# A long convolution as Toeplitz matmuls on one core: 128-row blocks against 64-row blocks in four tiles of the array

## The chip, the cores and the metric

The kernel runs on one core of a Trainium2 chip. The metric is the device time of one execution in microseconds (us), taken as the median of several runs. Three runs of the kernel before gave 2309.24, 2312.29 and 2312.61 us; the median is 2312.29 us.

## The reference

The input `x` has 32 batch entries, 64 channels (tokens of the later layers) and 1024 positions, all in fp32. Four residual layers follow each other. The first is the one that changes here: a state-space convolution along the 1024 positions, one filter per channel, with a mask by length.

```python
K = _get_kernel(log_dt, C, log_A_real, A_imag, Lq)      # one filter of 1024 taps per channel
y = irfft(rfft(u, n=2*Lq) * rfft(K, n=2*Lq)[None])[..., :Lq]   # causal convolution
y = y + u * D[:, None]
x = x + y * (arange(Lq)[None, :] < length[:, None])[:, None, :]
x = x + einsum('bsi,boi->bso', x, weight1[adapter_ids1])        # 1024 x 1024 weight per batch entry
x = x + einsum('bij,bkj->bik', x, weight2[adapter_ids2])        # the same with another table
x = x + lora_ffn(x)                                             # gate, up, silu, down, each with LoRA
```

## The kernel before, in words

The batch is cut into four chunks of eight entries. For every chunk the kernel runs sixteen adapter products (eight entries, two layers) and then the feed-forward layer. The convolution is done once, in the beginning, for all 32 entries: the part of chunk 0 is added to `x` in SBUF at once (L1419), the parts of the other chunks go to DRAM (`cd`, L1423) and are read back later.

**The filters.** The function `kernels(g)` makes the filters of a group of 4 or 8 channels from sines, cosines and exponentials on ScalarE, VectorE and GpSimd, and a small matmul (`pk`, L1346). ScalarE copies the result out (L1364) and stores it in a DRAM tile `kp` by a DMA on its own queue (L1366). Nine groups are made; the first two before the convolution starts, the others one at a time from within it, through `more()`, which `convolve` calls as `between()`.

**The convolution.** `convolve(kp, row, ha, between)` is called sixteen times, each for `HA = 4` channels. In this text a call is one of these sixteen. In a call, SyncE's queue (SP) first loads `uf`, the inputs of the four channels with the positions of a 128-block reversed (L1376). Then, for two channels at a time, it loads `hk` (L1385): 128 rows of 1024 numbers for each channel, read from `kp` in such a way that row p starts p numbers later. Every 128 columns of this table are one square Toeplitz block. The convolution of a channel is eight matmuls (L1404), one for each distance d between an output block and an input block: a 128 x 128 block as weights, and (8 - d) x 32 columns of `uf` as the moving operand, so 256, 224, ... 32 columns, all summed in PSUM. VectorE multiplies two channels' sums by the mask into `tmp` (L1172), GpSimd adds chunk 0's part to `x` and stores the rest.

**The weights that come early.** The adapters' weights come as 128 x 1024 tiles of 512 KB; chunk 0 needs 128 of them. While the convolution runs, SP also loads such tiles for chunk 0: `fetch(n)` issues the next n of them (L170). They go to places of their own (16 `early` tiles, 4 in the second `x` buffer, called `x_early`, and 7 `late` ones that open when the last filters are made) and to 9 rotating buffers `wa`, 36 in all. `fetch(8)` stands in the first call; later calls fetch one to two tiles each, 28 by the end, and the last eight are issued behind the last table. When the adapters begin, each rotating buffer is loaded again as soon as TensorE has used it.

**Order.** TensorE's order is the program's (it is scheduled by hand). SP's queue is in the order of the program too: the load of a `uf` buffer waits for the call two before, that of an `hk` buffer for the matmuls that last read it, and what stands behind it in the queue waits with it. The adapters of chunk 0 (L304) start when GpSimd has added the last call's result to `x`.

In the trace, an fp32 matmul stands as two instructions, each with its own weight load.

Of the kernel before, what the change touches and what calls it, by code (L numbers as in the profile page):

```python
# [9 lines left out]
F32 = mybir.dt.float32  # L10
# [9 lines left out]
P = 128  # L20
B, H, L = 32, 64, 1024
NS = 64
KT = L // P
# [8 lines left out]
MB = 4  # L32
MG = 2
NG = FM // MG
EARLY = 16
LEFT_AT = 11
LATE = 7
FIRST_LOADS = 8
MORE_LOADS = 3
ROTATING = 9  # L40
HA = 4
SEG = 2
# [10 lines left out]
KROW = P + L  # L53
# [23 lines left out]
def kernel(  # L77
# [55 lines left out]
    epool = first.enter_context(tc.tile_pool(name="epool", bufs=1, side="right"))  # L133
    early = [epool.tile([P, L], F32, tag=f"e{i}", name=f"early{i}") for i in range(EARLY)]
    early += [
# [995 lines left out]
def convolution(tc, cst, consts, xt, xf, ssm, lens, x0, cd, ps_tile, fetch, places):  # L1131
# [10 lines left out]
    nc = tc.nc  # L1142
    with ExitStack() as ctx:
# [5 lines left out]
        s3 = ctx.enter_context(tc.tile_pool(name="s3", bufs=3))  # L1149
# [14 lines left out]
        def small():  # L1164
            n_small[0] += 1
            return s1.tile([P, H], F32, tag=f"sm{n_small[0]}", name=f"sm{n_small[0]}")
# [4 lines left out]
        def tt(o, a, b, op):  # L1171
            nc.vector.tensor_tensor(o, a, b, op)  # L1172
            return o
# [80 lines left out]
        x, y = small(), small()  # L1254
# [6 lines left out]
        t, em, ep = small(), small(), small()  # L1261
# [110 lines left out]
        def convolve(kp, row, ha, between):  # L1372


            uf = s3.tile([P, HA, KT, B], F32, tag="uf", name=f"uf{ha}", bufs=2)
            nc.sync.dma_start(uf, xf[:, ha : ha + HA])  # L1376
            if ha == 0:
                fetch(FIRST_LOADS)
            tmp = g0_2.tile([P, HA, KT * B], F32, tag="tmp", name=f"tmp{ha}")
            for i in range(0, HA, 2):  # L1380
                hk = s3.tile([P, 2, L], F32, tag="hk", name=f"hk{ha + i}")

                for j in range(0, 2, 1 if ha == 0 else 2):
                    n = 1 if ha == 0 else 2
                    nc.sync.dma_start(  # L1385
                        hk[:, j : j + n],
                        bass.AP(
                            tensor=kps.tensor,
                            offset=kp[row + i + j : row + i + j + 1, 1:2].offset,
                            ap=[[1, P], [KROW, n], [1, L]],  # L1390
                        ),
                    )

                first, last = ha <= HA * MORE_LOADS, ha > H - HA * MORE_LOADS
                if ha and i == 0:
                    fetch(1 + first)
                elif ha and last:
                    fetch(1)
                if i:
                    between()  # L1400
                ps = ps_tile(f"pc{ha + i}").rearrange("p (i t) -> p i t", i=2)
                for j in range(2):
                    for d in range(KT):
                        nc.tensor.matmul(  # L1404
                            ps[:, j, d * B :],
                            hk[:, j, d * P : (d + 1) * P],
                            uf[:, i + j, : KT - d, :].rearrange("p k b -> p (k b)"),
                            start=(d == 0),
                            stop=(d == KT - 1),
                        )  # L1410
                tt(
                    tmp[:, i : i + 2, :],
                    ps,
                    maskf.unsqueeze(1).to_broadcast([P, 2, KT * B]),
                    ALU.mult,
                )
            xv = x0.rearrange("p k (b h) -> p k b h", h=H)[:, :, :, ha : ha + HA]
            tv = tmp.rearrange("p i (k b) -> p k b i", b=B)[:, :, :BC, :]
            nc.gpsimd.tensor_tensor(xv, xv, tv, ALU.add)  # L1419
            co = g0.tile([P, NCK - 1, HA * KT, BC], F32, tag="co", name=f"co{ha}")  # L1420
            tv = tmp.rearrange("p i (k c b) -> p c (i k) b", k=KT, b=BC)[:, 1:]
            nc.gpsimd.tensor_copy(co, tv)
            nc.gpsimd.dma_start(  # L1423
                cd.rearrange("c p g e -> p c g e")[:, :, ha // HA],
                co.rearrange("p c i b -> p c (i b)"),
            )
# [14 lines left out]
        maskf = mask.rearrange("p k b -> p (k b)")  # L1441
        for g, n in enumerate(GROUPS):
            h0 = sum(GROUPS[:g])

            def more():
                if len(ready) < min(g + 3, len(GROUPS)):
                    ready.append(kernels(len(ready)))
                    if len(ready) == len(GROUPS):
                        making.close()
                        places()  # L1450

            for i in range(0, n, HA):
                convolve(ready[g], i, h0 + i, more)
# [20 lines left out]
def _layouts(np, v):  # L1474
    cont = np.ascontiguousarray

    x = v["x"]

    xt = x.reshape(NCK, TC, KT, P).transpose(3, 0, 2, 1)

    xf = x.reshape(B, H, KT, P)[..., ::-1].transpose(3, 1, 2, 0)

    def states(a):
        return np.concatenate([a.T, a.T])
# [58 lines left out]
    for i, (m0, m1) in enumerate(BLOCKS):  # L1543
        n = 2 * (m1 - m0)
        ad[:, i, :, :n] = a[:, :, :, m0:m1].reshape(NE, P, n, R)
    left = left.reshape(P + REST, NE, R).transpose(1, 0, 2)
    n = 2 * BLOCKS[0][1]
# [71 lines left out]
```

## Time and profile before

| what | value |
|---|---|
| median of 3 runs | 2312.29 us |
| span of the profiled execution | 2313.8 us |
| TensorE busy | 2249.8 us (97%) |
| TensorE weight loads busy | 1868.0 us (81%) |
| DMA, mean over the span | 296 GB/s |
| first table `hk` issued | 25.14 us |
| adapters of chunk 0 begin in the chain of waits | 195.76 us |
| last adapter matmuls of chunk 0 end | 329.83 us |
| matmuls of the convolution (L1404) | 1024 instructions, 153.3 us busy |
| tables `hk` | 30 loads of 1024 KB and 4 of 512 KB |

The profiled execution's span is 1.5 us over the median of the runs. Times inside a stage are read from the start of this span. A busy TensorE isn't TensorE at its peak, since matmuls are pipelined and their ends are modelled; what a stage costs is read from its start and end, and from the wait that ends last in it.

### The profile page before, as it was taken

To read this page: it belongs to the slowest core of one execution; us is meant where nothing else is said; L and a number is where in the kernel's file an instruction comes from. 1 tells how busy PE (TensorE), PEld (TensorE's weight loads), DVE (VectorE), ACT (ScalarE), POOL (GpSimd) and SP (SyncE) were. 2 spreads that over 40 slices of the span, in tenths; PEclk is the share of its full clock that TensorE was granted. 3 is DMA by queue.
4 is the path that set the end of the run, shared out by engine and by line. 5 is a ranking of instruction groups with operands and counts; after the bars stand their busy time and mean duration, and the time that the engine had idled before them with its cause. 6 is when DMAs were issued, how large, how long until landed. Compare 5 with 4: busy or idle time off the path is not lost.

```text
span 2313.8 us, 53743 instructions
## 1 busy us (share of the span) xinstructions
PE 2249.8 (97%) x21706; PEld 1868.0 (81%) x21706; DVE 1320.6 (57%) x2791; ACT 380.0 (16%) x822; POOL 270.6 (12%) x388
## 2 busy tenths in 40 slices
PE   5999989999999999999999999999999999999999
PEld 4996557787777789688778889688769889799998
DVE  7511127567446776546535676646535676477585
ACT  4300001011001112111102212121102212121220
POOL 3423003111101121000000011000000011100000
PEclk9999999999999999999999999999999999999999
DMA  8999997879997957879997957879997947285582
GB/s 306 354 370 394 407 403 280 317 289 354 365 343 293 350 174 258 304 285 360 350 357 279 358 167 265 297 292 358 355 351 288 363 152 276 87 298 203 191 280 68
DMA packets 201802, 684.96 MB, mean 296 GB/s; under 512 B 26178, under 2 KB 28482, under 8 KB 201042
## 3 DMA queue, kind: packets, MB, share of 16 engines
q1 hardware_dynamic: 169714, 590.77, 69.5%
q0 software_dynamic: 25184, 82.37, 9.6%
q10 hardware_dynamic: 6656, 8.39, 1.0%
q8 instruction: 171, 2.80, 0.5%
q14 instruction: 77, 0.63, 0.1%
HBM read 614.02 MB, written 67.40 MB: 295 GB/s over the span
## 4 chain that ended last, share of the span: by engine, by line
PE 78%; DMA 14%; issue 5%; DVE 2%; POOL 1%; POOLq 0%; SPq 0%; ACT 0%; DVEq 0%
PE pq L664 28%; PE po L1063 22%; PE pa L304 11%; DMA wa<-in_w 7%; PE pc L1404 5%; PE pf L573 5%; PE pr L797 3%; DMA wa<-sums 2%; DMA sums<-kept 1%; PE pe L456 1%; DMA hk<-kp 1%; PE pl_d L427 1%; DMA kp<-ks 1%; DMA wf<-in_wg 0%; DMA wr<-in_wr 0%
## 5 line engine op out<-in xcount | busy, mean ns | idle before, releaser
L304 PE MATMUL pa<-wa,x 128*32 128x256 f32 x7760 | 449.1, 381 | 19.3 <-DMA wa<-in_w 16.8
L664 PE MATMUL pq<-xd,wa 128*128 128x128 f32 x3360 | 415.9, 275 | 1.3 <-DMA wa<-sums 0.9
L304 PEld LDWEIGHTS pa<-wa,x 128*32 128x32 f32 x7760 | 241.8, 110 | 209.9 <-DMA wa<-in_w 49.1
L664 PEld LDWEIGHTS pq<-xd,wa 128*128 128x128 f32 x3360 | 395.0, 192 | 2.3 <-DMA wa<-sums 2.2
L664 PE MATMUL pq<-xd,wb 128*128 128x128 f32 x2520 | 324.1, 276 | 0.6 <-DVE x L316 0.4
L664 PEld LDWEIGHTS pq<-xd,wb 128*128 128x128 f32 x2520 | 300.7, 192 | 4.7 <-DVE x L316 0.6
L314 DVE STREAM_TRANSPOSE y<-pa 128x512 f32<-128x512 f32 x64 | 45.9, 717 | 286.6 <-PE pa L304 286.6
L1063 PE MATMUL po<-act,wd 128*128 128x256 f32 x640 | 168.6, 386 | 0.0
L1404 PE MATMUL pc<-uf,hk 128*128 128x256 f32 (+7 forms) x1024 | 153.3, 312 | 12.2 <-DMA hk<-kp 9.5
L1063 PE MATMUL po<-actd,s 128*128 128x256 f32 x640 | 164.2, 379 | 0.0
L1063 PE MATMUL po<-actd,wd 128*128 128x256 f32 x640 | 164.2, 379 | 0.0
L1404 PEld LDWEIGHTS pc<-uf,hk 128*128 128x128 f32 x1024 | 148.4, 195 | 16.6 <-issue 7.9
L355 POOL DMA_INDIRECT bgu<-in_bgu,rows x44 | 51.4, 1168 | 924.0 <-PE pe L456 827.2
L573 PE MATMUL pf<-xd,wf 128*128 128x256 f32 x640 | 150.9, 381 | 0.0
L1063 PEld LDWEIGHTS po<-act,wd 128*128 128x128 f32 x640 | 117.8, 190 | 29.9 <-issue 14.6
L482 DVE TENSOR_TENSOR s<-wd 128x256 f32<-128x256 f32 x80 | 33.8, 423 | 184.1 <-PE po L1063 184.0
L573 PEld LDWEIGHTS pf<-xd,wf 128*128 128x128 f32 x640 | 121.2, 191 | 17.4
L1063 PEld LDWEIGHTS po<-actd,s 128*128 128x128 f32 x640 | 121.6, 190 | 16.5
L1063 PEld LDWEIGHTS po<-actd,wd 128*128 128x128 f32 x640 | 121.6, 190 | 16.5
L1095 ACT COPY uo<-po 128x256 f32<-128x256 f32 x48 | 17.9, 373 | 622.3 <-PE po L1063 620.2
L573 PE MATMUL pf<-xd,s 128*128 128x256 f32 x480 | 115.9, 385 | 3.9 <-DVE up L607 2.7
L573 PEld LDWEIGHTS pf<-xd,s 128*128 128x128 f32 x480 | 91.0, 191 | 20.0 <-DVE up L607 4.4
(235 smaller groups left out, 2566.4 us busy)
## 6 DMA issues: line engine op xcount, KB each, us to landing
wa<-in_w SPq DMA_DIRECT2D x485, 512.0 KB, 7.0
wa<-sums SPq DMA_DIRECT2D x210, 512.0 KB, 5.8
wb<-parts SPq DMA_DIRECT2D x120, 384.0 KB, 5.3
wd<-in_wd SPq DMA_DIRECT2D x80, 512.0 KB, 7.0
wb<-in_wq SPq DMA_DIRECT2D x90, 384.0 KB, 5.9
hk<-kp SPq DMA_DIRECT2D x30, 1024.0 KB, 8.8
sums<-kept POOLq DMA_DIRECT2D x30, 1024.0 KB, 7.2
wf<-in_wg SPq DMA_DIRECT2D x20, 512.0 KB, 7.1
```

The source lines that it names most:

```text
L304: nc.tensor.matmul(acc[i * S : (i + 1) * S, s * 256 : (s + 1) * 256], xs[c][:, kt, lo + s * S : lo + (s + 1) * S], wt[:, i * 256 : (i + 1) ...
L314: nc.vector.transpose(y, acc)
L355: nc.gpsimd.indirect_dma_start(out=t, out_offset=None, in_=table, in_offset=bass.IndirectOffsetOnAxis(ap=at_, axis=0),)
L427: nc.tensor.matmul(ps[pair(j)], at[:, i, pair(j)], x_i[:, 2 * H * j : 2 * H * (j + 1)], start=(i == 0), stop=(i == n - 1),)
L456: nc.tensor.matmul(ps[:, at_ * 2 * H : (at_ + 1) * 2 * H], bt[pair(j), g], tms[table][pair(j)], start=(g == 0), stop=True, skip_group_chec ...
L482: nc.vector.tensor_add(s1, a21, a22)
L573: nc.tensor.matmul(ps, ws[j][:, kt, :], xb[j][:, kt, :], start=start and kt == 0, stop=kt == KH - 1, skip_group_check=True,)
L664: nc.tensor.matmul(ps[:, to * TQ : (to + 1) * TQ], w[i][:, k, :], xb[:, j, SLOT[i], k, :], start=start and k == 0 and to == 0, stop=k == K ...
L797: nc.tensor.matmul(ps, wts[i][:, kt, :], xs[c][:, kt, :], start=(kt == 0), stop=(kt == KT - 1),)
L1063: nc.tensor.matmul(pss[j], *term, start=(s0 == m0 and i == 0 and home[j] % 2 == 0), stop=(end and i == len(terms) - 1 and not late), skip_ ...
L1095: nc.scalar.copy(u1, p1)
L1404: nc.tensor.matmul(ps[:, j, d * B :], hk[:, j, d * P : (d + 1) * P], uf[:, i + j, : KT - d, :].rearrange("p k b -> p (k b)"), start=(d == ...
```

## The change

A block becomes 64 x 64 numbers. A table `hk` now holds a pair of channels (`PAIR = 2`): rows 0 to 63 are one channel's table, rows 64 to 127 the other's, so that a channel's table has 64 rows of 1024 numbers instead of 128. It is loaded by two DMAs for each pair, one for each half of the rows. There are four such buffers of 4 KB per row instead of three of 8 KB. The input `uf` is laid out on the host to fit: its row halves hold the two channels, and for each the even and the odd 64-blocks apart.

For each pair the matmuls run over 16 distances e, two halves q of the output rows, and two channels r. A matmul has 64 rows of weights and 64 columns of weights and stands in one of four tiles of the array: r picks the row half, q the column half. The two channels' sums go to two PSUM banks (`banks[r]`), which hold both pairs of a call. There are 62 matmuls for a pair where there were 16. The mask products run for both banks at the end of the call.

The freed memory gives two more `early` tiles (18), so that 38 weights are held. `fetch(2)` stands in each call behind the first, ahead of the second pair's table; with `fetch(8)` in the first call that issues all 38 within the convolution.

```diff
-EARLY = 16
+EARLY = 18
-MORE_LOADS = 3
+PAIR = 2
+HP = P // PAIR
...
-            uf = s3.tile([P, HA, KT, B], F32, tag="uf", name=f"uf{ha}", bufs=2)
-            nc.sync.dma_start(uf, xf[:, ha : ha + HA])
+            uf = s3.tile([P, HA // PAIR, 2, KT * B], F32, tag="uf", name=f"uf{ha}", bufs=2)
+            nc.sync.dma_start(uf, xf[:, ha // PAIR : (ha + HA) // PAIR])
             if ha == 0:
                 fetch(FIRST_LOADS)
             tmp = g0_2.tile([P, HA, KT * B], F32, tag="tmp", name=f"tmp{ha}")
-            for i in range(0, HA, 2):
-                hk = s3.tile([P, 2, L], F32, tag="hk", name=f"hk{ha + i}")
-
-                for j in range(0, 2, 1 if ha == 0 else 2):
-                    n = 1 if ha == 0 else 2
+            halves = [slice(r * HP, (r + 1) * HP) for r in range(PAIR)]
+            banks = [ps_tile(f"pc{ha}_{r}").rearrange("p (i t) -> p i t", i=HA // PAIR) for r in range(PAIR)]
+            for i in range(HA // PAIR):
+                hk = s3.tile([P, L], F32, tag="hk", name=f"hk{ha}_{i}", bufs=4)
+                for r in range(PAIR):
+                    h = row + PAIR * i + r
                     nc.sync.dma_start(
-                        hk[:, j : j + n],
+                        hk[halves[r]],
                         bass.AP(
                             tensor=kps.tensor,
-                            offset=kp[row + i + j : row + i + j + 1, 1:2].offset,
-                            ap=[[1, P], [KROW, n], [1, L]],
+                            offset=kp[h : h + 1, HP + 1 : HP + 2].offset,
+                            ap=[[1, HP], [1, L]],
                         ),
                     )
-
-                first, last = ha <= HA * MORE_LOADS, ha > H - HA * MORE_LOADS
                 if ha and i == 0:
-                    fetch(1 + first)
-                elif ha and last:
-                    fetch(1)
+                    fetch(2)
                 if i:
                     between()
-                ps = ps_tile(f"pc{ha + i}").rearrange("p (i t) -> p i t", i=2)
-                for j in range(2):
-                    for d in range(KT):
-                        nc.tensor.matmul(
-                            ps[:, j, d * B :],
-                            hk[:, j, d * P : (d + 1) * P],
-                            uf[:, i + j, : KT - d, :].rearrange("p k b -> p (k b)"),
-                            start=(d == 0),
-                            stop=(d == KT - 1),
-                        )
+                for e in range(PAIR * KT):
+                    for q in range(PAIR):
+                        k0 = (e - q + 1) // 2 if e > q else 0
+                        if k0 == KT:
+                            continue
+                        for r in range(PAIR):
+                            nc.tensor.matmul(
+                                banks[r][halves[q], i, k0 * B :],
+                                hk[halves[r], e * HP : (e + 1) * HP],
+                                uf[halves[r], i, (q - e) % 2, : (KT - k0) * B],
+                                start=(e == 0),
+                                stop=(e == PAIR * (KT - 1) + q),
+                                skip_group_check=True,
+                            )
+            for r in range(PAIR):
                 tt(
-                    tmp[:, i : i + 2, :],
-                    ps,
-                    maskf.unsqueeze(1).to_broadcast([P, 2, KT * B]),
+                    tmp.rearrange("p (i r) t -> p r i t", r=PAIR)[:, r],
+                    banks[r],
+                    maskf.unsqueeze(1).to_broadcast([P, HA // PAIR, KT * B]),
                     ALU.mult,
                 )
...
-    xf = x.reshape(B, H, KT, P)[..., ::-1].transpose(3, 1, 2, 0)
+    xf = x.reshape(B, H // PAIR, PAIR, KT, 2, HP)[..., ::-1]
+    xf = xf.transpose(2, 5, 1, 4, 3, 0).reshape(P, H // PAIR, 2, KT * B)
```

## The prediction

> **What bounds the kernel now.** I read the page first. TensorE is busy nearly throughout, but the first fifteenth of the span is different: there the transfers are at their limit too. So I cut the first 330 us into stages and asked for each stage's busy times (last three columns: granted clock, DMA share, GB/s).
>
> ```profile
> PE 78%; DMA 14%; issue 5%; DVE 2%; POOL 1%; POOLq 0%; SPq 0%; ACT 0%; DVEq 0%
> ```
> ```profile
> 25.10:76.80 51.70, 43.41 (x311) 41.89 (x312) 39.55 (x67) 26.44 (x38) 28.05 (x35) 0.97 0.92 336
> 76.80:194.10 117.30, 114.16 (x844) 111.08 (x847) 26.03 (x42) 9.96 (x16) 30.69 (x37) 1.00 0.98 371
> 195.76:329.80 134.04, 123.32 (x2057) 67.94 (x2057) 21.98 (x36) 4.08 (x4) 15.92 (x28) 1.00 1.02 400
> ```
>
> Calls 4 to 15 fill 76.8 to 194.1: 117.3/12 = 9.77 us each, with TensorE busy for 114 of 117 us and the DMA share at 0.98. The adapters of chunk 0 follow, with the share at 1.02, and the end of that stage is a chain of loads. Pieces of the chain of waits in order of time, from both stages:
>
> ```profile
> 82.04 18.52 PE pc L1404 x128
> 100.55 0.62 PE pk L1346 x16
> ...
> 232.02 18.37 PE pa L304 x336
> ...
> 328.76 1.07 PE pa L304 x16
> ...
> 331.82 1.89 PE pl_g L427 x64
> ...
> 337.43 1.32 PE pe L456 x32
> 338.75 10.57 PE pf L573 x48
> ```
>
> In the calls matmul follows matmul; in the adapters a load of 9 to 12 us stands between them again and again. So from 25 to 330 us two things are nearly full at once. An edit here pays only if it takes work from DMA, and from TensorE as well where that sets the pace.
>
> **TensorE's part.** A channel now costs 16 instructions of the 128 in 18.52 us, 2.315 us; a pair 4.63, a call 9.26. After it, a pair has 62 matmuls, 124 instructions, in four tiles. Do four tiles run beside each other? L573, on the full array, needs 10.57/48 = 0.220 us for 256 columns. L304, in four column tiles, needs 18.37/336 = 0.0547, a quarter of it. L456, in four row tiles, puts 32 instructions with 128-column weights into 1.32 us, 0.041 each. So both directions run four abreast; two by two isn't in the trace, and I take it to behave alike.
>
> The pace of a tile: 4 x 54.7/256 = 0.855 ns a column. Of a channel's 16 instructions now, those of 256, 224, 192 and 160 columns need 2 x 832 x 0.855 = 1.42 us; the other eight share 0.89 us, 0.1115 each, which is the load of 128 weight columns. A load of 32 columns is bounded by L1346: 0.62/16 = 0.039. On the line between them a load of 64 columns costs 0.063. After it, a q = 1 tile runs 256, 256, 224, 224, ... 32, 32 columns, each twice: 4 x (1056 x 0.855 + 2 x 63) = 4.1 us a pair, 8.2 a call, 1.0 less than now; over sixteen calls 16 us of TensorE. If the two column tiles of a row half load one after the other, the short steps cost 2 x 0.063 each and the pair 4.8. L427 (four column tiles, 32-column weights, 1.89/64 = 0.030 each) speaks for loads side by side, so I take 4.1.
>
> The Trainium skill, TensorE: Matmul & The Clock Gate, Part 3, The mechanism, says that a weight load overlaps running matmuls only where the row group differs. By it the pair would be the 4.8, 0.2 more than now; no run here has two column tiles beside two row tiles.
>
> **The tables.** By bytes they halve: 64 loads of 256 KB for 64 channels' 512 KB, 16.8 MB less. At 371 GB/s a 512 KB table takes 1.41 us, all of them 90. A half-height one costs between 0.71 us (by bytes) and 1.41 (no gain from fewer rows). The trace has one like it: L1024 loads 256 KB into rows 64 to 127, and two gathers into rows 0 to 63 follow it. SP's instructions, then the stage windows:
>
> ```profile
> 1333.28 0.50 SPq L1024 DMA_DIRECT2D wl<-in_wd_rest  x1
> ```
> ```profile
> 1336.00:1337.00 1.00, 1.00 (x10) 0.97 (x9) 0.79 (x4) 0.27 (x1) 0.33 (x1) 1.00 1.00 225
> 1337.00:1338.00 1.00, 1.00 (x7) 0.87 (x6) 0.79 (x3) 0.00 (x0) 0.00 (x0) 1.00 0.98 238
> 1338.00:1339.00 1.00, 1.00 (x6) 0.90 (x5) 0.97 (x2) 0.00 (x0) 0.00 (x0) 1.00 1.01 242
> 1339.00:1340.00 1.00, 1.00 (x6) 0.87 (x6) 1.00 (x2) 0.68 (x1) 0.00 (x0) 1.00 1.05 258
> ```
>
> The engines are full and move 225 to 258 GB/s instead of 400. At those rates 256 KB takes 1.02 to 1.17 us, and full-height loads are in the mixture, so one alone is slower. I take 1.25, between 1.08 and 1.41. Then the tables need 64 x 1.25 = 80 us, only 10 less than now (bounds: 45 less, none).
>
> The Trainium skill, SBUF — State Buffer, Door 1: The DMA port swizzle, explains such a rate: 64 rows on one side of row 64 reach half of the memory's 16 ports, measured there at 196 GB/s for 1 MiB against 328. By that rule alone the tables would cost the same as now, and the sum below would be 10 us more.
>
> **What a call costs on DMA.** `uf` 1.41, four tables 5.0, two weight tiles 2.8, `cd` 384 KB 1.06: 10.3 us, against 8.2 on TensorE plus half of a filter's 0.87. So transfers set the pace, and TensorE's 16 us are hidden. They would show only with tables near 0.8 us.
>
> **Weights.** Two more `early` places change when tiles come, not how many: 128 for chunk 0 either way. But the order changes. Now eight loads stand behind the last table and keep the share at 1.0 until the adapters start. Afterwards nothing is left: the last table lands, then come a pair (4.1), two mask products (2 x 0.69, since both wait for the call's end), GpSimd's add (0.88) and the first tile's matmuls (0.88) before a buffer is free, and some 2 us until its load moves data (the first small load, `par`, took 2.4): 9 us, in which GpSimd's `cd` and LoRA loads, 1.2 MB or 3 us, still move. DMA loses 6 us there.
>
> **Instructions.** The q8 queue moved 2.80 MB for 43,412 TensorE instructions. There will be 32 pairs x 46 matmuls x 4 = 5,888 more, 0.38 MB, 1 us at 371 GB/s. Fetching 248 instructions in 4.1 us, 60 a us, is denser than L304's 37; L427's 128 in 1.89 us is as dense, but short.
>
> **Sum.** From 25 to 330 us on DMA: -10.2 + 6 + 1 = -3.2 us. Everything behind moves with it. 2313.8 becomes 2310.6; the span is 1.5 over the median of the runs, so the median becomes 2309. A measurement of this kernel can tell about 0.2%, 4.6 us, from no change.
>
> **Rival 1: bytes decide (faster).** If the two halves of a pair overlap, each using what the other leaves free, a table costs 0.71 to 0.8 us, a call 8.2 to 8.6 on DMA, and TensorE's 8.7 sets the pace: 12 x (9.77 - 8.7) = 13, some 5 in the first calls (the chain waits 9.05 us for a table at 61.17, about half of it bytes), 3 for two weight tiles fewer after the last call (1.31 each at 400 GB/s): 2291. For it: the halves are queued back to back, so an engine that is ahead of the others finds the other half free. Against it: the windows above.
>
> **Rival 2: SP's queue stalls on the filter stores (slower).** SP's waits between 25 and 196 us:
>
> ```profile
> SPq L1385 <- DMA kp<-ks: 11.6, 2, 8.7
> SPq L1376 <- DMA kp<-ks: 8.7, 2, 4.5
> SPq L170 <- DMA kp<-ks: 7.8, 1, 7.8
> ```
>
> L1376 and L170 read nothing of `kp`. Completions of the SP and ScalarE loads are counted in turn on eight semaphores, so SP waits for the eighth load before. At four loads a call a store is two calls back; at seven it is one. A store goes out 5.4 us into a call and lands 7.9 later (`kp<-ks` in the DMA issues), at 13.3; behind it SP holds the tables of the call after next, due at 9.1, while those need 5.8 to 8.7 to land. At 8.7 us a call that is 2 to 5 us of TensorE's waiting; at 10.3 it is hidden. It decides once stores land 1 us later than now, or ScalarE copies late. Five stores at 3 us, with the -3: 2321.
>
> **Rival 3: the tiles don't run four abreast.** Two at a time make a pair 8.2 us and a call 16.9: 16 x 7.1 = 114 more, less 6 for loads that then are all in time: 2420. It decides from 4.9 us a pair, where TensorE passes DMA's 10.3. L304 and L456 speak against it.
>
> **Rival 4: no effect at all** in the stage's length: 2312.
>
> **How the numbers follow.** The forecast has 0.37: its own range, with tables from 1.1 to 1.41 us, is 2300 to 2319, so faster by over 0.2% 0.15, within 0.16, slower 0.06. Rival 1 has 0.24, all faster. Rival 2 has 0.24: slower 0.21, within 0.03. Rival 3 has 0.10, slower. Rival 4 has 0.05, within. Faster 0.39, same 0.24, slower 0.37. The range leaves out a quarter of rival 1, an eighth of rival 2 and all of rival 3: 2287 to 2332.
>
> **What would show it.** Right: a pair's 124 instructions in about 4.1 us where nothing waits; TensorE idle in most calls, with tables as the releaser; the DMA share near 1 at clearly under 371 GB/s between 80 and 190 us; a hole in DMA before the first adapters; chunk 0's adapters ending within 5 us of 330. Wrong: calls back to back on TensorE (rival 1), SP waiting for `kp` in most of the pairs of calls (rival 2), or pairs of 5 us and more without a wait (rival 3).

## The result and the profile after

The changed kernel took 2337.49 us (median of four runs, 2331.86 to 2346.09) against 2312.03 us for the kernel before beside it (2309.24 to 2312.61): a ratio of 1.0119, with a 95% interval of 1.009 to 1.0149. It is slower by 25 us, where 2309 was forecast and the range ended at 2332. The profiled execution's span is 2339.9 us, 26.1 more than before.

All of the loss lies ahead of the adapters. They begin at 226.6 us instead of 195.8 and end at 357.5 instead of 329.8; their stage is 3.2 us shorter, and what follows is 1.5 us shorter. The stage windows, cut where the stages now begin and end (length; busy time and instructions of PE, PEld, DVE, ACT and POOL; then granted clock, DMA share and GB/s):

```profile
25.10:76.80 51.70, 39.66 (x962) 36.96 (x966) 36.37 (x65) 28.75 (x41) 25.25 (x31) 0.93 0.81 229
76.80:224.10 147.30, 117.55 (x3140) 109.60 (x3132) 24.81 (x48) 7.72 (x14) 32.68 (x41) 0.91 0.82 239
226.60:357.47 130.87, 122.00 (x2057) 68.76 (x2057) 21.14 (x30) 4.09 (x4) 15.96 (x28) 1.00 1.01 394
```

Before, this stretch was nearly full on both sides: DMA share 0.92 and 0.98, TensorE busy for 114 of 117 us. Now neither is full: the share is 0.82 and TensorE idles for 30 of 147 us. The instructions in order of time, TensorE's and then SP's (start, length, what, count, and in brackets the idle time just before):

```profile
47.41 4.25 PE L1405 MATMUL pc<-uf,hk 64*64 64x256 f32 x124
55.13 6.03 PE L1405 MATMUL pc<-uf,hk 64*64 64x256 f32 x124 [3.47 <-DMA uf<-in_xf]
...
88.69 6.32 PE L1405 MATMUL pc<-uf,hk 64*64 64x256 f32 x124 [9.43 <-issue]
...
199.95 4.42 PE L1405 MATMUL pc<-uf,hk 64*64 64x192 f32 x128 [1.99 <-issue]
205.32 8.64 PE L1405 MATMUL pc<-uf,hk 64*64 64x160 f32 x255 [0.95 <-issue]
```
```profile
61.33 8.78 SPq L1387 DMA_DIRECT2D hk<-kp  x2
...
72.72 2.75 SPq L171 DMA_DIRECT2D early<-in_w  x4
77.25 0.34 SPq L1377 DMA_DIRECT2D uf<-in_xf  x1
...
86.90 2.04 SPq L171 DMA_DIRECT2D early<-in_w  x3
90.15 0.34 SPq L1377 DMA_DIRECT2D uf<-in_xf  x1
```

Four things are to be seen. The first line is a pair without a wait: 124 instructions with starts from 47.41 to 51.44, as forecast. The second and third are pairs behind a wait for `uf`; they take 6 us, not 4 (for the third the view names no releaser, but the `uf` of 77.25 lands at 88.6, 11 us after its issue, and the pair starts at 88.69). SP's lines show why `uf` is late: four weight tiles, then three, go out ahead of it. And they show a second reason: within the line of 61.33, SP stands from 61.80 to 69.65 for a store of `kp`, and these weights and the `uf` go out behind it. And late in the stage the matmuls come in pieces of 128 and 255 with gaps of 1 to 2 us between them, for which the profile names nothing ("issue").

The slow pair is a matter of the clock. The windows of the matmuls alone (PE, PEld, clock, share, GB/s), a pair after work, a wait, and the pair after that wait:

```profile
47.40:51.50 4.10, 4.09 (x124) 3.92 (x124) 1.00 0.99 295
79.10:88.60 9.50, 0.16 (x6) 0.04 (x2) 0.68 1.00 316
88.70:94.80 6.10, 6.10 (x124) 6.04 (x124) 0.66 1.02 334
```

TensorE's waits, SP's waits (total, times, longest; the 25.4 us of "issue" hold the 9.4 us for `uf`), and the fetched instructions:

```profile
PE pc L1405 <- issue: 25.4, 16, 9.4
PE pc L1405 <- DMA uf<-in_xf: 6.8, 2, 3.5
PE pc L1405 <- DMA hk<-kp: 4.9, 2, 4.6
```
```profile
SPq L1387 <- DMA kp<-ks: 33.4, 4, 11.9
SPq L1387 <- PE pc L1405: 23.8, 8, 5.5
SPq L1377 <- PE pc L1405: 22.1, 6, 4.1
...
SPq L171 <- DMA kp<-ks: 3.7, 1, 3.7
```
```profile
q8 instruction: 194, 3.18, 0.6%
```

SP waits 37 us for `kp` now, 28 before. The 0.38 MB of additional instructions are just as forecast: 194 fetches of 16 KB where 2.80 MB were 171.

### The profile page after: what moved, and what is told of

Read it like the earlier page. It is cut to its first block, busy times and chain, and to the rows that moved or that the text cites. A ratio compares the mean times of both kernels' runs of the same rounds, so it can differ in the third digit from the quotient of the medians.

```text
span 2339.9 us, 59665 instructions
## 1 busy us (share of the span) xinstructions
PE 2247.0 (96%) x24650; PEld 1862.9 (80%) x24650; DVE 1316.2 (56%) x2791; ACT 380.5 (16%) x822; POOL 270.7 (12%) x388
## 4 chain that ended last, share of the span: by engine, by line
PE 78%; DMA 9%; issue 1%; DVE 1%; POOL 0%; POOLq 0%; SPq 0%; DVEq 0%
PE pq L665 28%; PE po L1064 23%; PE pa L305 13%; PE pf L574 7%; DMA wa<-in_w 6%; PE pr L798 3%; PE pe L457 2%; DMA wa<-sums 1%; DMA sums<-kept 1%; PE pl_d L428 1%; DMA wr<-in_wr 0%; PE pl_g L428 0%; PE pl_u L428 0%; PE po L1072 0%; PE pe_rest L457 0%
## 5 line engine op out<-in xcount | busy, mean ns | idle before, releaser
L1405 PE MATMUL pc<-uf,hk 64*64 64x128 f32 (+7 forms) x3968 | 153.2, 306 | 42.4 <-issue 25.4
L1405 PEld LDWEIGHTS pc<-uf,hk 64*64 64x64 f32 x3968 | 142.1, 141 | 52.9 <-issue 37.1
L1064 PEld LDWEIGHTS po<-act,wd 128*128 128x128 f32 x640 | 117.8, 190 | 30.0 <-issue 14.6
```

The lines of the kernel that those rows point to most:

```text
L1064: nc.tensor.matmul(pss[j], *term, start=(s0 == m0 and i == 0 and home[j] % 2 == 0), stop=(end and i == len(terms) - 1 and not late), skip_ ...
L1405: nc.tensor.matmul(banks[r][halves[q], i, k0 * B :], hk[halves[r], e * HP : (e + 1) * HP], uf[halves[r], i, (q - e) % 2, : (KT - k0) * B], ...
```

## The experiments

Theory 1 is the order on SP's queue, theory 2 the rate of loads into 64 rows, theory 3 the fetching of instructions, theory 4 the two more first weights. In the table, adapters' begin and end and the DMA share (from 25 us to their begin) are from the one profiled execution of each version, the ratio to the kernel before with its interval from the runs. Behind the adapters the profiled executions of these versions differ by up to 11 us (1973 in e10, 1984 in the kernel before), so a few us at the adapters' end needn't show in a ratio.

| run | begin | end | share | ratio |
|---|---|---|---|---|
| before | 195.8 | 329.8 | 0.96 | |
| after | 226.6 | 357.5 | 0.81 | 1.0119 (1.0090 to 1.0149) |
| e1 program's order | 221.2 | 351.7 | 0.84 | 1.0085 (1.0068 to 1.0102) |
| e2 weights of before | 226.2 | 360.4 | 0.78 | 1.0104 (1.0078 to 1.0130) |
| e4 order, two row tiles | 210.9 | 343.4 | 0.90 | 1.0086 (1.0069 to 1.0103) |
| e5 before, tables in halves | 263.1 | 397.9 | 1.01 | 1.0328 (1.0298 to 1.0357) |
| e7 the same, two queues | 253.9 | 386.9 | 0.99 | 1.0232 (1.0208 to 1.0257) |
| e10 order, gathers | 216.7 | 348.2 | 0.71 | 1.0067 (1.0047 to 1.0088) |
| e12 order, gathers from call 4 | 218.1 | 349.7 | 0.75 | 1.0075 (1.0050 to 1.0099) |
| e13 e12 with two row tiles | 199.2 | 330.8 | 0.83 | 1.0020 (1.0003 to 1.0037) |

**e1, the program's order.** Each load is queued behind the one that the program names before it.

```diff
+        def put(load):
+            with tc.issue_after(queue[-1]) if queue else ExitStack():
+                queue.append(load().ins)
-            nc.sync.dma_start(uf, ...)
+            put(lambda: nc.sync.dma_start(uf, ...))
-                        nc.sync.dma_start(hk[halves[r]], ...)
+                        put(lambda: nc.sync.dma_start(hk[halves[r]], ...))
-                    fetch(2)
+                    queue.append(fetch(2, queue[-1]))
```

> The changed kernel, with the loads on SP's queue held to the order in which the program names them: uf, both halves of the first table, two weight tiles, both halves of the second table, and so on. Nothing else is changed. Theory 1 (order): in the changed kernel the scheduler put the weight tiles on SP's queue in bunches of three to five ahead of the next call's uf; six waits of TensorE for uf or a table between 51 and 121 us add up to 27 us, and the slow clock after them costs 8 more. With the program's order those waits go: the adapters begin between 190 and 200 us instead of 226.6, the median is 2300 to 2313. Theory 2 (transfers of half height set the pace): the same bytes take the same time in any order, the waits move from uf to the tables; adapters at 218 to 227, median 2330 to 2340. Theory 3 (instruction fetch): the gaps of 0.5 to 2.3 us that end 1.3 to 1.6 us after a fetch packet stay as they are and show in the first 120 us too, 24 us in all; they alone keep the adapters from beginning before 192.

The waits for `uf` went, and the adapters began at 221, 5 us earlier, where theory 1 had 190 to 200. What came in their place, TensorE's waits from 25 to 230 us (total, times, longest):

```profile
PE pc L1415 <- issue: 27.3, 19, 2.8
PE pc L1415 <- DMA hk<-kp: 7.9, 6, 4.4
```

**e2, the weights of before** (`EARLY = 16`, one or two tiles a call, eight behind the last table).

> The changed kernel with the weights of before: 16 early places and the old rule for how many tiles a call fetches (28 within the calls, eight behind the last table). Tables, matmuls and the scheduler's freedom stay. Theory 4 (the two more first weights and the earlier fetch of all of them are the loss): median 2308 to 2318. Theory 1 (order): the scheduler bunches these weights as well, since nothing makes them wait, so the waits for uf stay: 2330 to 2342. Theory 3 says 2330 to 2342 too.

It gained nothing that can be told from the changed kernel. Theory 4 falls.

**e5 and e7, halves in the kernel before.** Nothing but the table loads differs from the kernel before, and in e5 SP's order is that of before.

```diff
-                    nc.sync.dma_start(hk[:, j : j + n], ... ap=[[1, P], [KROW, n], [1, L]])
+                    for r in range(2):
+                        nc.sync.dma_start(hk[r * 64 : (r + 1) * 64, j : j + n],
+                            ... ap=[[1, P // 2], [KROW, n], [1, L]])
```

> The kernel before, with each load of a table made as two, rows 0 to 63 and rows 64 to 127, one behind the other on SP's queue. Same bytes, same matmuls, same weights, and SP's order around them is that of before. Theory 2 (half height): 64-row packets took 1.6 times as long in the run with two row tiles (272 ns for 4352 bytes, against 168 by bytes); then a call's four tables need 5.6 x 0.6 = 3.4 us more, 9.77 becomes 13, the adapters begin 40 to 55 us later, median 2350 to 2370. Rival (only the greater number of loads counts, through the eight semaphores of rival 2): SP waits for kp more often, 2315 to 2330. Rival (half height costs nothing; order and instruction fetch alone are the loss): 2309 to 2318.

The window from 25 us to the adapters, and TensorE's longest item of waiting:

```profile
25.00:263.07 238.07, 180.37 (x1158) 171.79 (x1158) 63.10 (x109) 36.06 (x54) 57.40 (x72) 0.90 1.01 257
```
```profile
PE pc L1405 <- DMA hk<-kp: 51.3, 27, 4.4
```

The same bytes in halves cost 67 us more: the engines are full (1.01) and move 257 GB/s where they moved 360. DMA work is 1.01 x 238 = 240 us against 0.96 x 171 = 164, so a 512 KB table needs 76/64 = 1.19 us more than its 1.41, and one half of 256 KB about 1.3 us. That is direct evidence for theory 2, which had forecast less (40 to 55 us later, 2350 to 2370; the median is 2385). In e7 the second half goes out on ScalarE's queue.

> The kernel before, with each table load made as two of 64 rows, and rows 64 to 127 on ScalarE's queue: the two halves are in flight together. Theory 2 in its narrow form (a half-height load is slow only because both halves are not in flight at once): 2310 to 2325, 25 to 50 us less than with the two halves one behind the other. If half height is slow by itself: no less than with the halves one behind the other.

Two queues give back 9 of the 67 us in the profiles, and 19 of 72 in the medians (2385.2 to 2366.0; the kernel before beside them took 2313.4). Being in flight together isn't enough.

**e3, e6 and e10: three ways to bring both halves at once.** e3 makes one load of a pair's table, [2 channels][64 rows][1024]; e6 puts the second half on ScalarE's queue; e10 gathers 128 rows, each from a place of its own. All have e1's order.

```diff
-                for r in range(PAIR):
-                    ... put(lambda: nc.sync.dma_start(hk[halves[r]], ...))
+                nc.sync.dma_start(hk, bass.AP(..., ap=[[KROW, PAIR], [1, HP], [1, L]]))   # e3
+                nc.gpsimd.indirect_dma_start(out=hk, out_offset=None,                     # e10
+                    in_=bass.AP(tensor=kps.tensor, offset=0, ap=[[1, end + L], [1, 1]]),
+                    in_offset=bass.IndirectOffsetOnAxis(ap=rowat[:, pair : pair + 1], axis=0))
```

> As the kernel with the program's order on SP's queue, and besides each pair's table is one load into all 128 rows instead of two into 64 rows each: the same bytes, 32 table loads instead of 64, five loads a call instead of seven. Theory 2 (half height): a load into 64 rows takes 1.25 us where its bytes need 0.71, so 64 of them cost 35 us of transfer time too much; wherever transfers set the pace this comes back, 10 to 30 us less than with the program's order alone. Rival 2 of the prediction (the eight semaphores): fewer loads a call, so the filter stores are two calls back again and SP's waits for kp go, 0 to 10 us less. Theory 3 (instruction fetch): within 3 us of the program's order alone.

e3 took 2561.7 us, 1.106 of before. Its DMA share until the adapters is 0.33 at 110 GB/s, and TensorE waits for one table after the other. The Trainium skill, DMA: Bandwidth & Descriptors, Why a DMA increments its semaphore by 16 and not by 1, says that the size of the slowest dimension sets how many engines a load runs on; here that is 2. The run agrees in kind; it says nothing of theory 2.

> The changed kernel in the program's order on SP's queue, with the second half of each table (rows 64 to 127) issued by ScalarE on its own queue instead of by SP. Theory 2 (half height): loads of both halves now run at the same time and each uses what the other leaves free; the packets of the tables fall from 270 ns towards 170, the DMA share between 100 and 200 us falls from 0.9 to 0.7, the waits for hk go; adapters 5 to 15 us earlier than with the program's order alone (221). Theory 3 (instruction fetch): the 27 us of gaps behind instruction fetches are the rest of the loss and stay, unless they too come from full DMA engines, in which case they shrink with the share; adapters not before 200. If ScalarE's waits for a free buffer hold up the filters: more SP and TensorE waits for kp, and the adapters later than 221.

e6 was no gain: 1.0125 (1.0100 to 1.0150), adapters at 231.1. SP waited for `kp` for 40 us; ScalarE's queue also holds the filters.

> The changed kernel in the program's order on SP's queue, with each pair's table brought by one gather on GpSimd's queue (one index for each of the 128 rows) instead of two loads of 64 rows on SP's: the bytes are those of the change, but a load writes to both halves of the rows at once. Theory 2 (half height is slow because a load reaches only one half of the rows): packets of the tables take 160 to 185 ns instead of 270, DMA work before the adapters falls from 162 to 165 us of full share to 130 to 145, and with it the waits for tables; with Theory 3 (instruction fetch waits on full DMA engines) the fetch gaps shrink too. Adapters begin at 190 to 208, median 2300 to 2318. Rival (GpSimd: 32 gathers of 1.2 us in its queue, behind waits for free buffers, hold up its adds and the filters): tables or filters late, adapters at 215 or later, 2325 and more. If rows are slow for another reason than the half: packets stay at 270 ns.

The window of e10 up to the adapters, and TensorE's waits:

```profile
25.00:216.66 191.66, 151.32 (x4112) 139.24 (x4112) 62.56 (x115) 39.33 (x57) 91.20 (x108) 0.96 0.71 240
```
```profile
PE pc L1423 <- issue: 20.1, 14, 2.7
PE pc L1423 <- DMA hk<-kp,rowat: 9.4, 3, 4.7
```

This brings theory 2's rate back: DMA work is 0.71 x 192 = 136 us, as expected, against 165 in e1, and the median packet of GpSimd's queue, where the tables now are, takes 159 ns, where a table's packets of half height took 278 (4352 bytes, in e4); in e13 a gathered row of the same 4352 bytes takes 168. Yet the adapters begin at 216.7, only 4.5 us earlier. With DMA relieved, the gaps named "issue" remained. So half height alone isn't the loss either. The rival in the expectation, GpSimd's queue, had named 215 or later, and the number alone doesn't tell it from these gaps; e12 and e13 below do.

**e8, no transfers.** Only the first call loads tables, so the other channels' convolution isn't computed, and weights beyond eight come behind the last `uf`.

> The changed kernel in the program's order, with its transfers taken away: only the first call loads its tables, all later pairs run on those two, and the weights beyond the first eight are fetched behind the last uf. Left out: 60 of the 64 table loads, so the convolution of the other channels is not computed. Theory 3 as a matter of full DMA engines: the instruction fetches then take well under 1 us and TensorE's gaps go; calls at 8.2 to 8.8 us, adapters' start (as far as TensorE sets it) near 28 + 16 x 8.6 = 166. Theory 3 as a latency of the fetch itself, whatever the queues do: the gaps of 0.5 to 2 us remain, one for 256 instructions; calls at 9.5 to 10 us. Theory 2 alone: no gaps, 8.2 to 8.6 a call.

TensorE's matmuls (the stage's window from 84 to 168 us, and the end of the stage):

```profile
84.00:168.00 84.00, 84.00 (x2551) 80.19 (x2547) 18.34 (x30) 3.17 (x7) 28.43 (x37) 1.00 0.46 142
```
```profile
129.57 39.37 PE L1418 MATMUL pc<-uf,hk 64*64 64x256 f32 x1176
170.47 4.54 PE L1418 MATMUL pc<-uf,hk 64*64 64x160 f32 x128 [1.53 <-issue]
176.66 1.44 PE L1418 MATMUL pc<-uf,hk 64*64 64x128 f32 x60 [1.66 <-issue]
```

For 84 us there is no gap; then the weight loads set in (share 1.01 from 160 to 180 us), and the gaps are back at once, 128 matmuls apart. With their weight loads that is 256 instructions, one fetch of 16 KB. The fetch packets themselves hardly differ: between 50 and 190 us their median is 0.97 us here, 1.13 in the changed kernel, and 0.97 in e10, which has the gaps. In e12 one starts at 122.03 us, 0.7 us after TensorE ran out. That points to a wait ahead of the packet that grows with busy engines; no record shows where it waits.

**e4, e12 and e13: half the instructions.** Blocks of 64 rows by 128 columns use the two row tiles and no column tiles: 64 instructions a pair.

```diff
-                for e in range(PAIR * KT):
-                    for q in range(PAIR): ...
+                for d in range(KT):
+                    for s in range(2):
+                        for r in range(PAIR):
+                            nc.tensor.matmul(
+                                banks[r][:, i, d * B :],
+                                hk[halves[r], (2 * d + 1 - s) * HP : (2 * d + 3 - s) * HP],
+                                uf[halves[r], i, s, : (KT - d) * B], ...)
```

> As the kernel with the program's order on SP's queue, but the blocks are 64 rows by 128 columns: only the two row tiles, one per channel of the pair, no column tiles. A table row has 1088 numbers instead of 1024, and there are 17 early places instead of 18. A pair has 64 matmul instructions where the changed kernel has 124, and the same half-height tables. Theory 3 (instruction fetch): with half the instructions per microsecond the gaps behind the fetch packets go, and the pair takes 4.0 to 4.3 us since the weight load of one row half lies beside the other half's matmul: 10 to 20 us less than with the program's order alone. Theories 1 and 2: the pair is no faster than in four tiles, within 5 us of the program's order alone. If only the four tiles save time (two row tiles do not hide each other's loads), a pair takes 4.6 to 5.3 us and the stage is 8 to 20 us longer.

The gaps behind fetches are gone, but from the start of one pair to that of the next it takes 4.6 us where nothing waits, as on the full array: two row tiles save nothing. The stage is 10 us shorter than e1's, the median the same (2334.3 against 2333.6); behind the adapters e4's profiled execution took 6 us longer than e1's, within the spread named above. DMA is now near full again (0.90), and tables are what TensorE waits for.

e12 and e13 have the same transfers, half-height loads in the first three calls and gathers after, and differ in the tile form (and in one early place, and in table rows of 1088 numbers against 1024).

> The changed kernel in the program's order on SP's queue, with the tables of the first three calls as half-height loads on SP and those of the other thirteen as gathers on GpSimd's queue; 64 x 64 blocks in four tiles, 124 matmul instructions a pair. Against the run with gathers throughout it shows what the gathers in GpSimd's queue cost in the first calls (GpSimd stood 14 us behind a store of kp there): adapters begin 5 to 10 us earlier than 216.7, at 207 to 212. Theory 3 (instruction fetch): the gaps of 1 to 3 us behind fetches stay, 20 us or more between 100 and 210.

> The same transfers as in the run before it, but blocks of 64 rows by 128 columns in the two row tiles only: 64 matmul instructions a pair instead of 124, a pair 4.56 us instead of 4.1 where nothing waits, table rows of 1088 numbers, 17 early places. Theory 3 (the number of instructions, fetched through busy DMA engines): no gaps behind fetches, calls at 9.2 to 9.6 us, adapters begin at 185 to 198, 10 to 20 us earlier than with the four tiles although its matmuls take 15 us more. Rival (the gaps have another cause that the four tiles share): gaps as before, and the stage 5 to 15 us longer than with four tiles.

A window of e12 and a piece of TensorE's order in it, then the same of e13:

```profile
100.00:200.00 100.00, 80.02 (x2202) 73.23 (x2196) 12.35 (x20) 1.08 (x3) 39.95 (x47) 0.95 0.80 271
```
```profile
112.03 4.32 PE L1435 MATMUL pc<-uf,hk 64*64 64x192 f32 x127 [1.74 <-issue]
116.78 4.58 PE L1435 MATMUL pc<-uf,hk 64*64 64x192 f32 x128 [0.44 <-issue]
124.35 6.44 PE L1435 MATMUL pc<-uf,hk 64*64 64x192 f32 x209 [2.98 <-issue]
```
```profile
100.00:180.00 80.00, 80.00 (x1140) 78.29 (x1138) 12.36 (x20) 1.09 (x3) 36.24 (x42) 1.00 0.97 335
```
```profile
107.68 18.59 PE L1432 MATMUL pc<-uf,hk 64*128 64x256 f32 x256
126.87 18.59 PE L1432 MATMUL pc<-uf,hk 64*128 64x256 f32 x256
```

With 124 instructions a pair TensorE is busy for 80 of 100 us; with 64 for 80 of 80, and beside a fuller DMA (0.97). The adapters begin and end 19 us earlier, and the medians are 14.6 us apart (2329.3 and 2314.7), although the matmuls alone take 16 us more (32 pairs x 0.5). The trace of e12 ties the gaps to the fetches: between 110 and 206 us TensorE stops twelve times for more than 0.4 us, and each time it goes on 1.3 to 1.5 us after the end of a fetch packet. Theory 3 is shown. The gain of 4.1 against 4.63 us a pair, 17 us, is smaller than the 20 to 27 us of these gaps in e1 and e10. GpSimd's queue isn't the cause: e13 has the same gathers, and e12, without those of the first three calls, begins no earlier than e10 (207 to 212 had been expected).

**The rest.** e9 and e11 add the old rule of fetching to e1 and e10, to fill the hole before the adapters; e14 adds it to e13.

> The changed kernel in the program's order on SP's queue, with the old rule of fetching: 28 weight tiles within the calls, eight behind the last table, 16 early places. It tests the prediction's hole, the time in which DMA has little to do between the last table and the first adapters (share 0.51 from 200 to 220 us with the program's order). If the hole is worth the 6 us of the prediction: the eight tiles fill it, and the tables of the calls have one tile less beside them; adapters begin 3 to 8 us earlier than 221 and end about 6 us earlier than 351.7; median 6 to 12 us less than with the program's order alone (1.0085 of before), so 1.004 to 1.006. If instruction fetch alone sets the pace of the calls: adapters begin at 219 to 222 as before, and only the last stage differs, within 3 us.

> As the kernel with the gathers, with the old rule of fetching (28 tiles within the calls, eight behind the last table, 16 early places). If the gathers relieve DMA, the calls are no longer bound by transfers and the eight tiles fill the hole before the adapters: 3 to 8 us less than with the gathers alone, 2295 to 2312, a version at or below both kernels. If the gathers do not relieve DMA: as in the run with the old rule and half-height loads, 1.004 to 1.009 of before.

> The run with two row tiles and gathers, with the old rule of fetching (28 tiles within the calls, eight behind the last table, 16 early places). If TensorE is fed without gaps, the calls have transfers to spare and the hole before the adapters is filled: adapters begin at 183 to 196, end at 315 to 327 against 330 in the kernel before, median 2295 to 2310, 0.993 to 0.999 of before. If the calls are still held up by transfers or GpSimd's queue: 2312 to 2325.

None of the three gained: 1.0080 (1.0050 to 1.0110), 1.0066 (1.0043 to 1.0090), 1.0015 (1.0003 to 1.0027). Their adapters begin at 231.3, 216.9 and 202.0, none earlier than without the rule. Eight tiles moved from the calls into the hole seem only to be moved; the hole itself is real (share 0.17 from 219 to 226 us in the changed kernel).

e15 and e16 leave one and two more calls of e13 to SP.

> The version with two row tiles, the program's order and 17 early places, with the tables of the first four calls (instead of three) as half-height loads on SP, the others as gathers. If GpSimd's late gathers for the fourth call cost the time: TensorE's waits of 2.6 and 3.3 us between 60 and 82 us go with the slow clock after them; adapters begin at 191 to 196 instead of 199.2, median 2304 to 2311, 0.996 to 0.999 of before. If half-height loads are as late there: 2312 to 2320.

> The same with the tables of the first five calls as half-height loads on SP. The fifth call's half-height tables cost DMA 2 us more than gathers, in a stretch where its share is 0.8: within 3 us of the version with four calls, earlier only if GpSimd's queue is still late at the fifth call.

They came to 1.0029 (1.0017 to 1.0041) and 1.0026 (1.0016 to 1.0036), no better than e13. In e15's order of TensorE the wait stands ahead of the first gathered pair again:

```profile
83.13 7.69 PE L1432 MATMUL pc<-uf,hk 64*128 64x256 f32 x64 [9.02 <-issue]
```

Its gather went out at 76.40 us, behind a GpSimd add that had stood 5.5 us waiting for VectorE's mask product. In e16 that wait is gone, but TensorE waits 7.6 us in all for half-height tables, and the adapters begin at 198.2, 1 us earlier than in e13. So GpSimd's queue is late in the first calls, and half-height loads there are no better; what would be stays open. No version beat the kernel before.

## Why the prediction was wrong

**The pair in four tiles: right.** 4.10 us where nothing waits (4.1 forecast), so all four tiles run abreast, and column tiles don't wait for each other's loads. The 4.8 that the prediction drew from the rule of the Trainium skill on row groups (TensorE: Matmul & The Clock Gate, Part 3, The mechanism) isn't what the trace shows. Rival 3 falls. But TensorE's 16 us never appeared as busy time: it is 157.9 us from 25 us to the adapters, 158.1 before, since the mean clock fell from 0.99 to 0.92.

**The tables: a near miss.** A half was put at 1.25 us; e5 gives about 1.3. DMA work until the adapters is 0.81 x 201.6 = 163 us, 164 before. The forecast had taken 10 us off and put 1 on for instructions; two more weight tiles ahead of the adapters give back 2.6, and some 6 us are missing, 0.09 for each half. The rule of the Trainium skill, SBUF — State Buffer, Door 1: The DMA port swizzle, that rows on one side of row 64 reach half of the ports, made the tables cost the same as now, 1.41 a half; the 1.30 of e5 and the 1.34 that the measured work gives (1.25 + 0.09) lie between it and the prediction's 1.25. Rival 1, the halves helping each other out, falls with e5 and e7.

**The step that failed: "transfers set the pace, and TensorE's 16 us are hidden".** It took DMA for full, with 10.3 us a call, and added what was not hidden. DMA work came out nearly as summed, but 38 us of the 201.6 were idle on DMA, against 7 of 171 before, and of those only 6 are the hole that was foreseen (0.83 of 7 us). DMA and TensorE held each other up in turn: SP waits for a buffer that TensorE has not released (46 us in the two lines of SP's waits shown with the result), and TensorE then for a load that SP could not issue. The tables, which were to release TensorE in most calls, did so twice, for 4.9 us. Two terms were missing in it.

- *The order of SP's queue* was taken from the program. The scheduler writes it anew: weights wait for nothing, so it put three or four in a row ahead of `uf`, and from 112 us until the `late` places opened at 172 none went out (share 0.78). By e1 it is worth 5.8 us at the adapters' end; the runs' ratios, 1.0119 and 1.0085, point the same way, but their intervals overlap.
- *Instructions* were priced by bytes, 1 us. The bytes were right and the kind of price was wrong: what counts is that 256 instructions now last 4.2 us, and that a fetch behind busy engines isn't back in time. The prediction named the density, 60 a us, and then dropped it because L427 is as dense; L427 is over in 1.89 us, before one page is used up. With tables at full rate this term is 19 us (e12 against e13), net of the slower pair that e13 pays for it. The Trainium skill, Runtime: NRT & Kernel Launch, Instruction fetch mechanics, has the pages of 256 instructions, which the pieces of 128 matmuls agree with, and calls the crossing mostly hidden; with busy engines and this density it isn't.

Half height and fetches hide each other. Removing the fetch gaps alone (e1 to e4) moves the adapters' end by 8.3 us and the median by nothing; full-rate tables alone (e1 to e10) by 3.5; both (e1 to e13) by 21, although e4 and e13 give up the four tiles' faster pair. So the 27.6 us at the adapters' end, in one profiled execution of each, are 5.8 for the order, 21 for these two together, and 0.9 that remain.

**Rival 2** was the nearest in number, 2321, and in sign (its own terms, five stores at 3 us on top of the forecast, make 2324). It isn't cleared. SP did wait for `kp` for 37 us in place of 28, and one of these waits, 61.80 to 69.65, lies ahead of the late `uf` of 77.25, so part of that loss may be its. In e1 SP still waits 22 us for `kp`, and TensorE's waits for tables, the only ones for SP's loads that the profile names there, come to 7.9 us in all: with the queue in order it can hardly cost more than that and the slower clock behind such waits. No run takes the waits for `kp` away alone, so its share in the changed kernel stays open.

Of what would show it, the pair held, the DMA share near 1 and the adapters' end did not, and the share of 0.82 at 239 GB/s is the first sign that no resource set the pace.

## What to carry to other kernels

A sum over one resource holds only while that resource is full; look for the lookahead that keeps it full, and ask what the queue's order will be when loads that wait for nothing are added. Price instructions by how long a page of 256 lasts beside how busy the DMA engines are, not by their bytes. Halving a tile's rows halves its bytes, but not its time.

## What the runs showed of the hardware

- An instruction fetch comes late beside data. At about 60 TensorE instructions a us and a DMA share of 0.7 to 0.8, gaps of 0.4 to 4.3 us come at most once in 256 instructions (e12); at a share of 0.46 there were none in 84 us (e8); at 28 a us there were none in 80 us even at 0.97 (e13).
- A gather into 128 rows from overlapping places in DRAM, 4 KB a row, takes 159 ns a packet (e10), as the 4 KB packets of the kernel before do, and costs GpSimd about 1 us an issue.
- In a wait of 9.5 us the granted clock was 0.68, in the pair behind it 0.66, and that pair took 6.1 us in place of 4.1. Behind the wait of 3.5 us at 51.7 the clock was 0.72 and the pair 1.8 us longer.
- Two row tiles, with 128-column weights, take as long as the full array (4.6 us a pair); four tiles with 64-column weights take 4.1.
